# Hybrid attention and feed-forward layer on one core: the first batch element's moments, preparations, row sums and scores are placed elsewhere

## The chip, the cores and the metric

The kernel runs on one core of a Trainium2 chip. The metric is the device time of one execution in microseconds (us); the median of three runs before the change is 4003.38 us. The engines are called PE (TensorE), DVE (VectorE), ACT (ScalarE), POOL (GpSimd) and SP (SyncE, which here only issues transfers).

## The reference

The input x has 8 batch elements of 512 tokens and 256 features. Four residual layers follow each other, each on the layer norm of x:

```python
x = x + attn_a(layernorm(x))   # per token: attention between the 64 places of each of 16 heads
x = x + ffn(layernorm(x))
x = x + attn_b(layernorm(x))   # causal attention over the 512 tokens
x = x + ffn(layernorm(x))      # the same weights again

def attn_a(x):                 # H, C = 16, 64
    Q, K, V = x @ Wq + bq, x @ Wk + bk, x @ Wv + bv      # each reshaped to (b, s, H, C), Q / sqrt(C)
    scores = einsum('bshq,bshk->bshqk', Q, K)            # masked to k <= q
    w = softmax(scores)
    return einsum('bshqk,bshk->bshq', w, V).reshape(b, s, H * C) @ Wo + bo
```

The change is in attn_a of the first batch element. For every token and head, the 64 outputs are quotients of two row sums over a triangle of 64 x 64 scores: the sum of exp(q k) v, over the sum of exp(q k).

## The kernel before

**Tiles and units.** 128 tokens lie on the 128 partitions, so a batch element b has four token tiles i. Four heads (256 columns) make a column group g, so there are 16 groups (g, i) per batch element, taken with g outermost. The triangle of each head is cut into its diagonal and into squares of 32, 16, 8, 4, 2 and 1; these make four units u of work per group:

- unit 0: the 32-squares of two heads; unit 2: those of the other two heads. Scores (L784) are made by POOL from the copies kt of K and Q in SBUF.
- unit 1: the 16-squares of four heads. Scores are made by DVE, into the tile w16, of which there is one buffer.
- unit 3: all smaller squares, scores by DVE, into the tile ws, one buffer.

Units 0 and 2 use tiles w, three buffers. A unit's scores are two instructions of 128x1024 (four smaller ones in unit 3).

**Steps.** The class AttentionA lays the units of all batch elements in one list, and step(n) issues, in one fixed order, what is due at step n for several units: scores of unit n (`scores`), exponentials of unit n-1 on ACT (`exps`, L798), the product with v of unit n-2 on DVE (`weigh`, L808), a transfer that adds one half of the tile to the other (`halve`, issued by POOL, L814; not for unit 3), a further halving on POOL for units 0 and 2 (`fold`, L819), the row sums on DVE (`gather`, L845, into tiles red), and their addition on POOL into the group's sums acc (`add_rows`, L852). `small_squares` (L835, L852) adds the 2- and 1-squares. Then come the reciprocal on DVE (`invert`, L856), the product with it on POOL (`divide`, L860), the transposes and the output projection on PE. Within a group of four steps, the order that matters here is this (k is the step modulo 4; three parts to a step, separated by yields):

- k = 0: weigh unit 2; POOL's scores of unit 0, with the transfer of unit 2 between their two instructions; the reciprocal; then divide and the fold of unit 0.
- k = 1: weigh unit 3, gather unit 1; then scores of unit 1, add_rows, small_squares, fold of unit 2; then gather unit 0.
- k = 2: weigh unit 0; POOL's scores of unit 2 with unit 0's transfer between; later gather unit 2, then gather unit 3.
- k = 3: weigh unit 1 and its transfer; then scores of unit 3.

Each of PE, DVE, ACT and POOL executes in exactly this program order (a manual schedule); SP's transfers are placed by a scheduler. The first batch element's 64 steps have no other work beside them. From step 75 on, the feed-forward layers and the second attention of batch element b-1 (generator `after_a`) are issued between the parts of the steps of element b, in proportion to estimated costs.

**The start.** x of element 0 is loaded first. Then follow the rows last_qv and last_k and the weights of the column groups (fitted). `fit_qkv(g)` subtracts the last row from the weights (L344, L346; by DVE for g = 0, by POOL otherwise), puts the bias into their last row by a small transfer, and stores them in DRAM, from where `load_w` fetches them for every later group. `measure(b)` takes the four tiles' moments on DVE (L524, L525) and their scales on POOL (L529 to L532). The generator `later_weights` prepares what later layers need: a bias in three bfloat16 parts (ACT L421, L422; POOL L423; DVE L428), the scaled w3 (L451), wbqk and wbvp with their last rows subtracted (L456), their stores, and a bound on the scores (`bound_scores`: squares on ACT L373 and L374 of sqv and sk, 96 products on PE L382, a norm on ACT L388 and DVE L390). One piece of it is issued after each part of a step. Its tiles, like last_qv, last_k and the weights of groups 1 to 3, come from one pool of seven blocks of 1 MB (`block`), a block being free again after its last use.

```python
wt = ctx.enter_context(tc.tile_pool(name="wt", bufs=1))
hp = ctx.enter_context(tc.tile_pool(name="hp", bufs=7))
ps_f = ctx.enter_context(tc.tile_pool(name="ps_f", bufs=5, space=bass.MemoryType.PSUM))
```

Of the kernel before, what the change touches and what calls it, by code (L numbers as in the profile page):

```python
# [9 lines left out]
F32 = mybir.dt.float32  # L10
# [3 lines left out]
ALU = mybir.AluOpType  # L14
AX = mybir.AxisListType

P = 128
# [9 lines left out]
GW = GH * C  # L27
NG = HID // GW
# [256 lines left out]
def fast_path(ctx: ExitStack, tc: tile.TileContext, k, t, flag):  # L285

    nc = tc.nc
    ident = k.ident
# [7 lines left out]
    ap_ = ctx.enter_context(tc.tile_pool(name="ap", bufs=2))  # L296
# [42 lines left out]
    def fit_qkv(g):  # L339

        wqv, wk = fitted[g]
        eng = nc.vector if g == 0 else nc.gpsimd
        qv_last = last_qv[:, g * 2 * GW : (g + 1) * 2 * GW].unsqueeze(1).to_broadcast([P, DC, 2 * GW])
        eng.tensor_tensor(wqv, wqv, qv_last, ALU.subtract)  # L344
        k_last = last_k[:, g * GW : (g + 1) * GW].unsqueeze(1).to_broadcast([P, DC, GW])
        eng.tensor_tensor(wk, wk, k_last, ALU.subtract)  # L346
        nc.sync.dma_start(wqv[P - 1 : P, DC - 1, :], t.b_qv[g : g + 1, :])
        nc.sync.dma_start(wk[P - 1 : P, DC - 1, :], t.b_a[1:2, g * GW : (g + 1) * GW])
        nc.sync.dma_start(wqv_d[g].rearrange("p (c f) -> p c f", c=DC), wqv)
        nc.sync.dma_start(wk_d[g].rearrange("p (c f) -> p c f", c=DC), wk)  # L350
# [206 lines left out]
    def squares(unit):  # L557

        off = 0
        for n, h0, nh in unit:  # L560
            nsq = nh * C // (2 * n)
            yield n, off, nsq, slice(h0 * C, (h0 + nh) * C)
            off += nsq * n * n
# [40 lines left out]
    class AttentionA:  # L604
# [33 lines left out]
        def step(self, n):  # L638

            weighed = self.at(n - 2)  # L640
            if weighed[0] is not None:
                self.weigh(*weighed)
            unit = self.at(n)
            on_pool = unit[3] in (0, 2)
            if on_pool:
                half = self.scores(*unit)
                next(half)
            if weighed[0] is not None:
                self.halve(*weighed)
            if on_pool:  # L650
                next(half, None)
            b, i, g, u = self.at(n + 40)
            if u == 0 and g == 0 and i == 0 and b > 0:
                self.x[b] = load_x(b)
            b, i, g, u = self.at(n + 10)
            if u == 0 and g == 0 and i == 0:
                self.measure(b)
            b, i, g, u = self.at(n + 8)
            if u == 0 and g == 0:
                self.live["xn"] = normed(self.x[b][:, i, :], *self.rn[b, i], "a")  # L660
            b, i, g, u = self.at(n - 5)
            if u == NU - 1:
                self.invert(b, i, g)
            b, i, g, u = self.at(n - 4)
            if u == 1:
                self.gather(b, i, g, u)
            b, i, g, u = self.at(n + 7)
            if u == 0 and g == 0:
                nc.scalar.copy(self.live[b, i], self.live.pop("ps_ln"))
            if self.at(n - 1)[0] is not None:  # L670
                self.exps(*self.at(n - 1))
            yield
            if unit[0] is not None and not on_pool:
                for _ in self.scores(*unit):
                    pass
            for args in self.sums:
                self.add_rows(*args)
            self.sums = []
            b, i, g, u = self.at(n - 5)
            if u == NU - 1:  # L680
                self.divide(b, i, g)
            b, i, g, u = self.at(n - 2)
            if u == NU - 1:
                self.small_squares(b, i, g)

            b, i, g, u = self.at(n - 4)
            if u == 0:
                self.fold(b, i, g, u)
            b, i, g, u = self.at(n - 3)
            if u == 2:  # L690
                self.fold(b, i, g, u)
            b, i, g, u = self.at(n - 9)
            if u == NU - 1:
                self.new_x(b, i, g)
            b, i, g, u = self.at(n + 2)
            if u == 0:
                self.keep_qk(b, i, g)
            b, i, g, u = self.at(n - 7)
            if u == NU - 1:
                self.turn_group(b, i, g)  # L700
            b, i, g, u = self.at(n - 8)
            if u == NU - 1:
                self.project_out(b, i, g)
            b, i, g, u = self.at(n + 3)
            if u == 0:
                self.project(b, i, g)
            yield
            b, i, g, u = self.at(n - 4)
            if u == 2:
                self.gather(b, i, g, u)  # L710
            b, i, g, u = self.at(n - 5)
            if u == 0:
                self.gather(b, i, g, u)
            b, i, g, u = self.at(n - 3)
            if u == NU - 1:
                self.gather(b, i, g, u)
            b, i, g, u = self.at(n - 7)
            if u == NU - 1:
                nc.scalar.copy(self.live["att"], self.live.pop("pta"))
            b, i, g, u = self.at(n + 8)  # L720
            if u == 0 and g == 0:
                self.live[b, i] = lnp.tile([P, DC, P], F32, tag="xnt_a", name=f"xnta_{b}_{i}", bufs=NT)
                self.live["ps_ln"] = turned_over(self.live.pop("xn"), half_bank().rearrange("p (c s) -> p c s", c=DC))
            yield
# [40 lines left out]
        def scores(self, b, i, g, n_u):  # L765

            qv, kt = self.live[b, i, g][:2]
            if n_u == 0:
                acc = ap_.tile([P, 2, GW], F32, tag="acc", name=f"acc_{b}_{i}_{g}", bufs=3)
                self.live[b, i, g].append(acc)  # L770
                nc.vector.tensor_tensor(acc[:, 0, :], qv[:, 0], kt[:, 0], ALU.mult)

            if n_u in (0, 2):
                w = wt.tile([P, 4096], F32, tag="w", name=f"w_{b}_{i}_{g}_{n_u}", bufs=3)
            elif n_u == 1:
                w = wt.tile([P, 4096], F32, tag="w16", name=f"w16_{b}_{i}_{g}")
            else:
                w = wt.tile([P, 2 * SMALL], F32, tag="ws", name=f"ws_{b}_{i}_{g}")
            self.live[b, i, g, n_u] = w
            eng, q = (nc.gpsimd, kt[:, 1]) if n_u in (0, 2) else (nc.vector, qv[:, 0])  # L780
            for n, off, nsq, cols in squares(units[n_u]):
                for e, ev, rows, columns in pieces(w, n, off, nsq, cols):
                    shape = list(e.shape)
                    eng.tensor_tensor(  # L784
                        e, rows(q).to_broadcast(shape), columns(kt[:, 0]).to_broadcast(shape), ALU.mult
                    )
                    yield
# [50 lines left out]
        def gather(self, b, i, g, n_u):  # L838


            w = self.live.pop((b, i, g, n_u))
            for n, off, nsq, cols in squares(units[n_u]):
                if n > 2:
                    red = ap_.tile([P, 2, nsq * n], F32, tag=f"red{nsq * n}", name=f"red_{b}_{i}_{g}_{n_u}_{n}", bufs=2 + (n < 32))
                    nc.vector.tensor_reduce(red, self.columns_of(w, n, off, nsq), AX.X, ALU.add)  # L845
                    self.sums.append((b, i, g, n, cols, red))

        def add_rows(self, b, i, g, n, cols, part):

# [1 line left out]
            rows = acc[:, :, cols].rearrange("p a (x t) -> p a x t", t=2 * n)[..., n:]  # L851
            nc.gpsimd.tensor_tensor(rows, rows, part.rearrange("p a (x i) -> p a x i", i=n), ALU.add)  # L852

        def invert(self, b, i, g):
            acc = self.live[b, i, g][2]
            nc.vector.reciprocal(acc[:, 0, :], acc[:, 0, :])  # L856

        def divide(self, b, i, g):
            acc = self.live[b, i, g][2]
            nc.gpsimd.tensor_tensor(acc[:, 1, :], acc[:, 1, :], acc[:, 0, :], ALU.mult)  # L860

        def turn_group(self, b, i, g):
            acc = self.live.pop((b, i, g))[2]
# [477 lines left out]
    with tc.manual_schedule(engines={ET.PE, ET.DVE, ET.Activation, ET.Pool}):  # L1341
        a = AttentionA()
        prep = later_weights()
        fit_qkv(0)
        weights = None
        done, spent = after_a(), 0
        for n in range(-10, a.steps):
            for part, _ in enumerate(a.step(n)):
                if n >= 2:
                    next(prep, None)  # L1350
                while 3 * spent * each < total * (3 * (n - each - 11) + part + 1):
                    spent += next(done)
            if 0 <= n < NG - 1:
                fit_qkv(n + 1)
        for _ in done:
            pass
    judge()
# [86 lines left out]
```

## Time and profile before

| | us |
|---|---|
| runs | 4002.61, 4003.38, 4004.08; median 4003.38 |
| the profiled execution | 4009.55 |
| its span, first to last instruction | 4007.6 |
| first reciprocal (L856) | 86.2 |
| second | 141.4 |
| from the second on, spacing in the first batch element | 23.7 |
| sixteenth, the last of the first batch element | 475.6 |
| spacing of the later ones, mean of 111 | 28.7 |

There are 128 reciprocals, one per group, so their spacing shows the pace of the kernel. Busy time is given per engine; transfers are counted apart. A duration is that of one instruction from its start to its end, and instructions of one engine overlap a little at their ends, so that the next one can start before the last has ended: what an instruction costs its engine is read from start to start.

### The profile page before, as it was taken

What the parts mean: (1) busy time and instruction counts of PE and PEld (TensorE: products, weight loads), DVE (VectorE), ACT (ScalarE), POOL (GpSimd) and SP (SyncE); (2) the same over time, 40 slices, a digit from 0 to 9 for tenths busy, and PEclk for the clock granted to TensorE, in tenths of its full rate; (3) what the DMA queues carried; (4) which work ended last, traced back from release to release, by engine and by line L of the source; (5) the groups of instructions that cost most, each with busy time, mean ns of one, the idle gap of its engine ahead of it and who ended that gap; (6) DMA issues with size and microseconds to landing.
All of it is one profiled execution on the core that took longest, in us unless ns stands there. A gap on an engine that the chain in (4) does not pass through costs nothing.

```text
span 4007.6 us, 37678 instructions
## 1 busy us (share of the span) xinstructions
PE 2958.0 (74%) x12328; PEld 2012.2 (50%) x12328; DVE 3376.7 (84%) x3777; ACT 2337.2 (58%) x3145; POOL 3098.1 (77%) x3051
## 2 busy tenths in 40 slices
PE   1543478777876888768787788768787778768988
PEld 0311145355653656346553566346653556436847
DVE  4899988998889888998989988998889988897115
ACT  2433465666755766666755767567656667555342
POOL 6688888887888887887888888888888878886211
PEclk7555689888987989889897889879898899879999
DMA  8566777668776777668776688668877687767304
GB/s 240 114 141 145 146 182 182 147 161 199 199 162 126 195 188 196 150 147 210 174 192 139 168 198 214 147 131 198 195 181 151 154 199 205 155 133 210 126 29 167
DMA packets 118653, 671.07 MB, mean 167 GB/s; under 512 B 12704, under 2 KB 31915, under 8 KB 43824
## 3 DMA queue, kind: packets, MB, share of 16 engines
q0 software_dynamic: 78336, 570.46, 62.9%
q1 hardware_dynamic: 40112, 98.11, 6.8%
q8 instruction: 100, 1.64, 0.2%
q14 instruction: 105, 0.86, 0.1%
HBM read 255.90 MB, written 9.96 MB: 66 GB/s over the span
## 4 chain that ended last, share of the span: by engine, by line
DVE 38%; PE 16%; POOL 14%; DMA 12%; issue 8%; ACT 8%; POOLq 0%; DVEq 0%; ACTq 0%
DVE red L845 15%; DMA w<-w 12%; DVE w L808 10%; PE ph L1120 5%; ACT w L798 3%; POOL w L819 3%; DVE ws L808 3%; POOL w L784 3%; PE pqkb L1167 3%; DVE ws L784 3%; POOL acc L852 3%; DVE w L784 2%; POOL w L814 2%; DVE acc L856 2%; POOL h L1036 2%
## 5 line engine op out<-in xcount | busy, mean ns | idle before, releaser
L798 ACT ACTIVATE w<-w 128x2048 f32<-128x2048 f32 x384 | 734.2, 1913 | 653.8 <-POOL w L784 440.8
L1120 PE MATMUL ph<-h,hidden 128*128 128x512 f32 x4096 | 1047.9, 412 | 77.4 <-POOL h L1036 45.5
L784 POOL TENSOR_TENSOR w<-k 128x1024 f32<-128x1024 f32 x512 | 1076.2, 2102 | 9.6 <-ACT k L762 9.0
L1120 PEld LDWEIGHTS ph<-h,hidden 128*128 128x128 f32 x4096 | 795.3, 196 | 282.1 <-POOL h L1036 55.9
L808 DVE TENSOR_TENSOR w<-w,qv 128x1024 f32<-128x1024 f32 x768 | 899.8, 1213 | 22.4 <-ACT w L798 22.3
L845 DVE TENSOR_REDUCE red<-w 128x128 f32<-128x1024 f32 (+1 forms) x384 | 601.8, 1567 | 171.6 <-DMA w<-w 94.6
L819 POOL TENSOR_TENSOR w<-w 128x1024 f32<-128x1024 f32 x256 | 643.1, 2512 | 72.5 <-DMA w<-w 71.9
L814 POOL DMA_DIRECT2D w<-w x384 | 337.1, 878 | 339.7 <-issue 134.8
L852 POOL TENSOR_TENSOR acc<-acc,red 128x256 f32<-128x256 f32 (+1 forms) x640 | 471.0, 736 | 152.3 <-DVE red L845 124.5
L845 DVE TENSOR_REDUCE red<-ws 128x256 f32<-128x2048 f32 (+1 forms) x256 | 435.5, 1743 | 0.0
L746 PE MATMUL qv<-wqv,xnta 128*128 128x512 f32 x512 | 299.3, 715 | 89.9 <-DVE ws L808 82.4
L808 DVE TENSOR_TENSOR ws<-ws,qv 128x1024 f32<-128x1024 f32 (+3 forms) x512 | 294.7, 638 | 49.4 <-ACT ws L798 49.4
L1052 PE MATMUL pw<-xnt,gate 128*128 128x512 f32 (+2 forms) x1152 | 298.8, 419 | 24.9 <-ACT silu L1028 18.0
L784 DVE TENSOR_TENSOR w<-qv,k 128x1024 f32<-128x1024 f32 x256 | 301.3, 1219 | 3.6
L784 DVE TENSOR_TENSOR ws<-qv,k 128x1024 f32<-128x1024 f32 (+3 forms) x512 | 299.8, 648 | 0.0
L868 PE MATMUL bank<-ident,acc 128*128 128x128 f32 x256 | 64.3, 341 | 287.5 <-ACT k L761 287.1
L798 ACT ACTIVATE ws<-ws 128x1920 f32<-128x1920 f32 x128 | 231.5, 1809 | 75.3 <-DVE ws L784 74.7
L1052 PEld LDWEIGHTS pw<-xnt,gate 128*128 128x128 f32 x1152 | 227.6, 213 | 82.1 <-ACT silu L1028 22.3
L1229 ACT ACTIVATE eb<-psb 128x256 f32<-128x256 f32 (+3 forms) x512 | 182.2, 443 | 146.6 <-PE psb L1226 146.3
L1146 PE MATMUL pof<-w,h 128*128 128x256 f32 x1024 | 247.9, 396 | 19.4 <-ACT h L1085 19.4
L1085 ACT ACTIVATE h<-ph,s_sb 128x512 fp32r<-128x512 f32 (+1 forms) x256 | 171.1, 688 | 145.9 <-PE ph L1120 144.6
L856 DVE RECIPROCAL acc<-acc 128x256 f32<-128x256 f32 x128 | 223.2, 1744 | 12.3 <-POOL acc L852 12.3
(143 smaller groups left out, 4723.5 us busy)
## 6 DMA issues: line engine op xcount, KB each, us to landing
w<-w POOLq DMA_DIRECT2D x384, 1024.0 KB, 7.7
hidden<-in_h POOLq DMA_DIRECT2D x128, 1024.0 KB, 7.9
gate<-in_w12p POOLq DMA_DIRECT2D x32, 1024.0 KB, 9.0
w<-w_d SPq DMA_DIRECT2D x16, 1024.0 KB, 12.0
wqv<-wqv_d SPq DMA_DIRECT2D x31, 512.0 KB
wo<-in_wo SPq DMA_DIRECT2D x32, 256.0 KB, 7.4
wbqk<-wbqk_d SPq DMA_DIRECT2D x8, 1024.0 KB
w<-in_h SPq DMA_DIRECT2D x8, 1024.0 KB, 7.0
```

Source lines behind the costliest of these rows:

```text
L746: nc.tensor.matmul(qv.rearrange("p j f -> p (j f)"), xnt[:, c, :], wqv[:, c, :], start=(c == 0), stop=(c == DC - 1),)
L784: eng.tensor_tensor(e, rows(q).to_broadcast(shape), columns(kt[:, 0]).to_broadcast(shape), ALU.mult)
L798: nc.scalar.activation(e, e, AF.Exp, scale=C**-0.5)
L808: nc.vector.tensor_tensor(ev, e, columns(qv[:, 1]).to_broadcast(list(e.shape)), ALU.mult)
L814: nc.gpsimd.dma_start(w[:, :2048], w[:, 2048:], accum_op=ALU.add)
L819: nc.gpsimd.tensor_tensor(w[:, :1024], w[:, :1024], w[:, 1024:2048], ALU.add)
L845: nc.vector.tensor_reduce(red, self.columns_of(w, n, off, nsq), AX.X, ALU.add)
L852: nc.gpsimd.tensor_tensor(rows, rows, part.rearrange("p a (x i) -> p a x i", i=n), ALU.add)
L856: nc.vector.reciprocal(acc[:, 0, :], acc[:, 0, :])
L1052: nc.tensor.matmul(pj[:, toks], w[:, m % 4, j, c, :], xs[:, p, c, toks], start=(p == 0 and c == 0), stop=(p == 1 and c == DC - 1),)
L1120: nc.tensor.matmul(pss[j], w[:, j, c, :], h_in(p, c), start=(p == 0 and c == 0), stop=(p == 1 and c == MC - 1),)
L1146: nc.tensor.matmul(po, h(0, c)[:, i * P : (i + 1) * P], w3[:, c, :], start=(c == 0), stop=False)
```

## The change

- `measure(0)` is issued ahead of `fit_qkv(0)`, and no longer at step -10.
- `fit_qkv` of the groups 1, 2 and 3 is issued after the steps 3, 13 and 23 instead of 0, 1 and 2; the pieces of `later_weights` are issued from step 5 on instead of step 2.
- For batch element 0 (`alone`), the scores of unit 1 are made by POOL from kt.
- For batch element 0, `sum_up` adds the row sums in PSUM: five products with the identity on PE, of acc and of the four tiles red. `invert` and `divide`, now both on DVE, read them there.
- The tiles red hold the sums of all four heads for one size of square, so those of units 0 and 2 go into one tile of 128x256, with one buffer; the three other sizes have three buffers. For the other batch elements POOL adds both halves in one instruction, so that there are four additions of red in a group and not five.

```diff
@@ step
             b, i, g, u = self.at(n + 10)
             if u == 0 and g == 0 and i == 0:
-                self.measure(b)
+                if b > 0:
+                    self.measure(b)
...
             if u == 0:
                 self.project(b, i, g)
+            b, i, g, u = self.at(n - 4)
+            if u == NU - 1 and self.alone(b):
+                self.sum_up(b, i, g)
             yield
@@ scores
             eng, q = (nc.gpsimd, kt[:, 1]) if n_u in (0, 2) else (nc.vector, qv[:, 0])
+            if n_u == 1 and self.alone(b):
+                eng, q = nc.gpsimd, kt[:, 1]
@@ gather
                 if n > 2:
-                    red = ap_.tile([P, 2, nsq * n], F32, tag=f"red{nsq * n}", name=f"red_{b}_{i}_{g}_{n_u}_{n}", bufs=2 + (n < 32))
-                    nc.vector.tensor_reduce(red, self.columns_of(w, n, off, nsq), AX.X, ALU.add)
-                    self.sums.append((b, i, g, n, cols, red))
+                    if n_u != 2:
+                        self.live["red", n] = ap_.tile(
+                            [P, 2, GW // 2], F32, tag=f"red{n // 32}", name=f"red{n}_{b}_{i}_{g}", bufs=1 if n == 32 else 3
+                        )
+                    red = self.live["red", n]
+                    part = red[:, :, cols.start // 2 : cols.stop // 2]
+                    nc.vector.tensor_reduce(part, self.columns_of(w, n, off, nsq), AX.X, ALU.add)
+                    if n_u != 0 and not self.alone(b):
+                        self.sums.append((b, i, g, n, slice(0, GW), red))
@@ new, and invert and divide
+        @staticmethod
+        def alone(b):
+
+            return b == 0
+
+        def sum_up(self, b, i, g):
+
+            sums = ps_f.tile([P, 2, GW], F32, tag="pf", name=f"sums_{b}_{i}_{g}")
+            nc.tensor.matmul(sums, ident, self.live[b, i, g][2], start=True, stop=False)
+            for n in (32, 16, 8, 4):
+                rows = sums.rearrange("p a (x t) -> p a x t", t=2 * n)[..., n:]
+                red = self.live["red", n].rearrange("p a (x i) -> p a x i", i=n)
+                nc.tensor.matmul(rows, ident, red, start=False, stop=n == 4)
+            self.live[b, i, g].append(sums)
+
         def invert(self, b, i, g):
-            acc = self.live[b, i, g][2]
-            nc.vector.reciprocal(acc[:, 0, :], acc[:, 0, :])
+            acc, *sums = self.live[b, i, g][2:]
+            nc.vector.reciprocal(acc[:, 0, :], sums[0][:, 0, :] if sums else acc[:, 0, :])
 
         def divide(self, b, i, g):
-            acc = self.live[b, i, g][2]
-            nc.gpsimd.tensor_tensor(acc[:, 1, :], acc[:, 1, :], acc[:, 0, :], ALU.mult)
+            acc, *sums = self.live[b, i, g][2:]
+            if sums:
+                nc.vector.tensor_tensor(acc[:, 1, :], sums[0][:, 1, :], acc[:, 0, :], ALU.mult)
+            else:
+                nc.gpsimd.tensor_tensor(acc[:, 1, :], acc[:, 1, :], acc[:, 0, :], ALU.mult)
@@ the main loop
         prep = later_weights()
+        a.measure(0)
         fit_qkv(0)
...
             for part, _ in enumerate(a.step(n)):
-                if n >= 2:
+                if n >= 5:
                     next(prep, None)
...
-            if 0 <= n < NG - 1:
-                fit_qkv(n + 1)
+            if n in (3, 13, 23):
+                fit_qkv(n // 10 + 1)
```

## The prediction

> **What bounds the kernel now.** I read the page first, then busy time by stage, then one period of the first batch element in order of time.
>
> ```profile
> span 4007.6 us, 37678 instructions
> PE 2958.0 (74%) x12328; PEld 2012.2 (50%) x12328; DVE 3376.7 (84%) x3777; ACT 2337.2 (58%) x3145; POOL 3098.1 (77%) x3051
> DVE 38%; PE 16%; POOL 14%; DMA 12%; issue 8%; ACT 8%; POOLq 0%; DVEq 0%; ACTq 0%
> ```
>
> No engine is full over the whole span, so the stages have to be read apart. The change acts in the first two: the start, and the rest of the first element's attention, which has no feed-forward work beside it. The columns are the stretch, its length, then busy us (count) of PE, PEld, DVE, ACT and POOL, the granted clock, the DMA share and GB/s.
>
> ```profile
> 52.00:92.00 40.00, 5.90 (x12) 2.96 (x12) 25.82 (x27) 10.51 (x10) 38.95 (x37) 0.54 0.98 287
> 92.00:113.00 21.00, 2.94 (x14) 2.92 (x14) 0.32 (x1) 5.85 (x6) 1.88 (x1) 0.50 0.55 151
> 150.00:500.00 350.00, 139.55 (x245) 66.08 (x246) 349.38 (x361) 138.09 (x142) 305.05 (x268) 0.56 0.68 141
> ```
>
> From 150 to 500 us DVE is idle for 0.6 of 350 us: DVE bounds this stage. A group (four steps) takes 23.72 us, the spacing of the reciprocals (L856) from 141.4 us on; the sixteenth is at 475.6. From 92 to 113 us everything waits for one load:
>
> ```profile
> ACT sk L374 <- DMA sk<-in_wqkv: 21.9, 1, 21.9
> ```
>
> One stretch of the periodic stage, in order of time (start, duration, engine, line, out<-in; other rows left out):
>
> ```profile
> 311.31 2.28 DVE L845 TENSOR_REDUCE red<-w 128x256 f32<-128x2048 f32 x1
> ...
> 313.62 2.36 DVE L784 TENSOR_TENSOR w<-qv,k 128x1024 f32<-128x1024 f32 x2
> 313.73 0.81 POOL L852 TENSOR_TENSOR acc<-acc,red 128x256 f32<-128x256 f32 x1
> 314.42 0.69 POOL L835 TENSOR_TENSOR ws<-ws 128x256 f32<-128x256 f32 x1
> 315.19 1.66 POOL L852 TENSOR_TENSOR acc<-acc,ws 128x256 f32<-128x256 f32 x2
> ...
> 316.80 2.36 POOL L819 TENSOR_TENSOR w<-w 128x1024 f32<-128x1024 f32 x1
> ...
> 317.35 2.34 DVE L808 TENSOR_TENSOR w<-w,qv 128x1024 f32<-128x1024 f32 x2
> ...
> 319.61 1.21 DVE L845 TENSOR_REDUCE red<-w 128x128 f32<-128x1024 f32 x1
> ```
>
> Rows 1 and 2: DVE reduces unit 1's tile w16 and at once refills it with the next group's scores; w16 has one buffer. The last reduce needs POOL's fold of unit 2, which ends at 316.80 + 2.36 = 319.16, only 0.45 us before DVE starts on it. DVE leads, but POOL is close behind in this one place.
>
> **What the Trainium skill says.** GPSIMD Engine Reference, 3.1 Elementwise: a two-input operation takes 1.96 times as long as on VectorE; here a score piece advances POOL by 1.92 us and DVE by 1.13, 1.7 times. TensorE: Matmul & The Clock Gate, Architectural detail, calls ACT, DVE and GPSIMD strict FIFOs; the trace agrees in that every period repeats one order per engine, so what is put ahead of the fold delays the fold. DMA: Bandwidth & Descriptors, Issuing engines are not separate DMA queues: transfers from any engine share the 16 DMA engines; 52 to 92 us agrees, with share 0.98 while SP's and POOL's transfers run together. Perfetto Trace Analysis, Optimization Strategy: "Consistent bubbles" can mean that there isn't room for the next tile; before, DVE has none here. I expect them after.
>
> **Periodic stage, by work.** Steps from start to start. DVE loses unit 1's scores (313.62 to 315.90, 2.28) and gains the product that was L860 on POOL (the PSUM-reading 128x256 product L805 advances DVE by 0.33): 23.72 - 1.95 = 21.77. POOL has one gap of 2.68 us in a period (before the DMA issue at 303.21), so 21.04 of work; it gains 2 x 1.92 = 3.84 and loses five adds (3.7) and the product L860 (0.69): about 20.5. By work alone DVE would still bound, at 21.77.
>
> **Periodic stage, by waits.** In the step with unit 1, scores come first in POOL's part, ahead of small_squares and the fold of unit 2. Now they are POOL's, and write w16, so they wait until DVE's reduce of the group before has ended (311.31 + 2.28 = 313.59). From there: 0.07 to start (the add at 117.30 came 0.07 after its reduce), scores 3.84, L835 0.77, two adds 1.61, fold 2.35: it ends 8.64 after the reduce, at 322.23. DVE, rid of its scores, would want it after 1.12 + 0.33 + 2.26 = 3.7 us, at about 317.3. Stall: 4.9 us a period.
>
> The loop closes on DVE: reduce of unit 2 1.13, of unit 3 3.32, weighing of unit 1 2.26, scores of unit 3 2.26, weighing of unit 2 2.26, L771 0.33, reciprocal 1.66, product 0.33, weighing of unit 3 2.20, reduce of unit 1 2.28; sum 18.03; with POOL's 8.64 and 0.03 to start, **26.70 us against 23.72: +2.98 a group**. The queue behind the waiting POOL instruction is the small squares, the fold, unit 2's scores and the DMA issue; DVE waits for the fold. Unit 2's exponentials, next in line, would end some 4 us before they are used. The trace doesn't show POOL's price for the 16x16 shape: at least 1.82, at most the 2.10 that a whole piece of unit 0 or 2 is recorded with, so 26.5 to 27.1; I take 1.92, as the piece has as many elements and the same innermost run of 8.
>
> Groups: unit 1 is POOL's for 16 groups, which gives 15 such waits; the first two fall before the twelfth step, in the start counted below. 13 x 2.98 = **+38.7**; the last interval, without the wait but with the lighter DVE, gives back 1.
>
> **Sums on TensorE.** A 128x512 product with the identity 1.04 us, four of 128x256 at 0.66: 3.7 us a group. PE is busy 140 of 350 us, and between the end of DVE's last reduce (324.14) and the reciprocal (331.3) lie 7 us, of which the two last products need 1.3. Cost 0; were PE's cover gone, 3.7 less those 7, still 0. Reading sums from PSUM: L805 (0.41, PSUM) and its like L771 (0.42) cost the same; up to 0.1 a group. The PSUM pool's five buffers are hardly used here.
>
> **Other batch elements.** One add for both halves of the 32-squares: 112 adds of 0.69 us (77 us of POOL) go, but on the chain they carry 2.3 us, in five of 112 groups, so at most -2.3; the single buffer costs nothing, as at least 10.1 us lie between the add and the next write (rows L852 and L845 in order of time). I take -1, bounds -2.3 and +1.
>
> **The start.** Moments: x is there at 2.98, the four pairs take 2.2 us and POOL's scaling 2.0, all under DVE's 10.4 us wait for wqv. But projection then waits for the fitted weights' bias row, issued on SP at 17.11; with some 2 us to land (x needs 2.5), it starts at about 19.5 instead of 22.43: -2.9. Then three fits (3 x 3.7 on POOL) no longer stand ahead of unit 2's scores. My run by hand: k at 25.0, unit 0's scores to 28.9, unit 1's to 32.7, unit 2's to 37.5, exponentials to 39.5: DVE's first weighing of unit 2 at 39.6 instead of 50.95, **-11.3** (the 2.9 is in it). Each moved fit also issues on SP two bias rows and stores of 0.5 and 0.25 MB; the loads of the stored weights come at steps 9, 25 and 41, the fits at 3, 13 and 23, so at least six steps of some 6 us lie between: cost 0.
>
> The preparations come later and cost again. Their six casts and three subtractions alternate between ACT and POOL and hold DVE up for about 9 us. last_qv, last_k and two fit blocks now stay until steps 13 and 23, so of the seven blocks three are left for four: wbvp must wait for w3's store before it can load. SP and POOL queue behind: I count 8 us of waiting on POOL for w3 and wbvp. rows, w3, wbqk, wbvp, their stores and the squares move 8.75 MB at some 260 GB/s, beside 1 MB for each halving, so sk lands near 118 us and holds ACT at step 10 (before: 107 us, at step 7). The second reciprocal comes at about 127.6 instead of 141.4: **-13.8**, all of the above included. After it fall the norm's wait (L390, 3.98, and two table loads of 1.28: 5 net) and the second fit (3.7 less 2.3 of slack: +1.4); the third hides in POOL's gap. Start: **-7.4**, bounds -25 (all stalls overlap) and +15 (each block is waited for in turn).
>
> **Sum.** -7.4 + 38.7 - 1 - 1, less 1 for a hiccup of 2.1 us near 400 us that the bubbles absorb: **+28**. The profiled execution took 4009.55 us (its span 4007.6 and 1.95 around it), 6.2 above the median 4003.38; +28 gives 4037.6 there and **4031** as a median.
>
> **Rivals.** *The lighter DVE wins:* if unit 1's scores did not wait, or the fold came in time, the period would be 21.77: 16 x -1.95 = -31, with the start -38, 3965 us. For it: POOL's work does fit. Against it: w16's one buffer and the fold's 0.45 us. It decides at a fold ending 3.7 us after the reduce, 8.64 by my count. 9%. *The start gets worse* by the shortage of blocks: +15 for -7.4, 4054 us; for it, the load of sk already stalls for 21.9 us. 14%. *The start absorbs it:* most of the old 31.5 us between the first two reciprocals (55.2 less 23.7) and the 11.3 vanish: -38, with +36 after it, about 4001. The full DMA share speaks against it. 9%. My forecast, 68%.
>
> **Numbers.** 0.2%, 8 us, is about what a measurement of this kernel tells from no change. Faster by more: the first rival and a little of the third, 0.10; within: 0.08; slower: 0.82. Range 4010 to 4052: the start's bounds and the shape's price, short of the two far cases.
>
> **What will show it.** After, DVE's reduces (L845) wait for POOL's fold (L819) by about 5 us once a group in the first element, reciprocals stand 26.7 apart, POOL's scores wait for DVE's reduce, and nothing waits for TensorE's sums. The second reciprocal lies near 128 us. I am wrong if the reciprocals stand at 21.8, or if the fold isn't what DVE waits for.

## The result and the profile after

The changed kernel is slower: 4045.36 us (median of four runs, 4043.04 to 4055.76) against 4003.73 us, ratio 1.0101, 95% interval 1.0074 to 1.0129. Forecast were 4031 us, in a range from 4010 to 4052. The profiled execution took 4043.04 us, its span is 33.7 us longer than that of before. The page of the changed kernel (whose line numbers are higher from line 657 on) has these lines for those shown of before:

```profile
span 4041.3 us, 37835 instructions
PE 2994.3 (74%) x12488; PEld 2034.5 (50%) x12488; DVE 3348.9 (83%) x3761; ACT 2336.3 (58%) x3145; POOL 3083.0 (76%) x2875
DVE 34%; POOL 22%; PE 17%; DMA 11%; issue 9%; ACT 8%; SPq 0%; POOLq 0%; ACTq 0%; DVEq 0%
```

DVE and POOL both have less to do, and still the kernel is longer: POOL's share of the chain has risen from 14% to 22%. Busy time by stage, columns as before (the busy us of DVE is the third of the five pairs, that of POOL the fifth):

```profile
92.00:113.00 21.00, 0.69 (x2) 0.29 (x2) 6.78 (x6) 2.44 (x3) 14.37 (x12) 0.50 0.51 164
150.00:500.00 350.00, 176.26 (x382) 95.21 (x382) 286.28 (x313) 123.69 (x126) 281.09 (x191) 0.66 0.62 130
```

In the stage that DVE filled to 349.38 of 350 us it now sits idle for 64 us. One period there, in order of time:

```profile
311.30 3.40 DVE L856 TENSOR_REDUCE red<-w 128x256 f32<-128x2048 f32 x2
...
313.65 3.86 POOL L790 TENSOR_TENSOR w<-k 128x1024 f32<-128x1024 f32 x2 [1.26 <-DVE red L856]
...
317.47 0.61 POOL L841 TENSOR_TENSOR ws<-ws 128x256 f32<-128x256 f32 x1
...
318.16 1.66 POOL L864 TENSOR_TENSOR acc<-acc,ws 128x256 f32<-128x256 f32 x2
...
319.78 2.34 POOL L825 TENSOR_TENSOR w<-w 128x1024 f32<-128x1024 f32 x1
...
322.15 1.22 DVE L856 TENSOR_REDUCE red<-w 128x128 f32<-128x1024 f32 x1 [4.86 <-POOL w L825]
```

The brackets give an engine's idle time and who ended it. POOL's scores of unit 1 wait for DVE's reduce of the tile that they overwrite (here the row's first 2.28 us); the small squares and the fold of unit 2 queue behind them; DVE waits 4.86 us for the fold. The waits from 150 to 500 us have it in twelve groups, ten times with 4.9 us, once each with 4.6 and 2.7 (the thirteenth, of 0.7 us, is for another fold); the columns are us in total, times, and the longest:

```profile
DVE red L856 <- POOL w L825: 56.7, 13, 4.9
POOL w L790 <- DVE red L856: 18.3, 12, 4.5
```

The reciprocals divide the spans. Traces of all runs, in us (the tail is from the last reciprocal on):

| kernel | third reciprocal at | third to sixteenth | sixteenth to last | tail |
|---|---|---|---|---|
| before | 165.1 | 310.5 | 3212.8 | 319.2 |
| before, once more | 160.4 | 310.5 | 3218.3 | 319.3 |
| changed | 172.4 | 346.4 | 3201.1 | 321.3 |
| scores_last | 172.5 | 333.6 | 3202.0 | 322.6 |
| scores_dve | 164.8 | 317.4 | 3203.1 | 321.6 |
| old_start | 177.1 | 345.9 | 3208.2 | 318.0 |
| old_start_last | 176.0 | 334.6 | 3203.6 | 316.3 |
| start_only | 171.3 | 313.9 | 3214.2 | 319.1 |
| prep_later_only | 148.8 | 310.5 | 3222.9 | 320.7 |
| merge_only | 162.5 | 310.5 | 3201.8 | 319.7 |
| two_adds_late | 162.4 | 310.7 | 3203.2 | 322.0 |
| merge_prep | 147.0 | 310.5 | 3197.6 | 320.8 |
| scores_last_no_transfer | 169.6 | 301.5 | 3208.0 | 321.6 |

So the 33.7 us of the changed kernel are +7.3, +35.9, -11.7 and +2.1. The two traces of before lie 4.7 us apart at the third reciprocal and 5.5 us apart in the long stretch, so a difference of that size between two single traces shows nothing. The ratios below compare medians with runs of before taken along with each experiment; those gave 4011.04, 4011.14 or 4011.84 us.

### The profile page after: what moved, and what is told of

Read it like the earlier page. It is cut to its first block, busy times and chain, and to the rows that moved or that the text cites. A ratio compares the mean times of both kernels' runs of the same rounds, so it can differ in the third digit from the quotient of the medians.

```text
span 4041.3 us, 37835 instructions
## 1 busy us (share of the span) xinstructions
PE 2994.3 (74%) x12488; PEld 2034.5 (50%) x12488; DVE 3348.9 (83%) x3761; ACT 2336.3 (58%) x3145; POOL 3083.0 (76%) x2875
## 4 chain that ended last, share of the span: by engine, by line
DVE 34%; POOL 22%; PE 17%; DMA 11%; issue 9%; ACT 8%; SPq 0%; POOLq 0%; ACTq 0%; DVEq 0%
DVE red L856 13%; DMA w<-w 10%; DVE w L814 9%; POOL w L790 5%; PE ph L1150 5%; POOL w L825 5%; POOL acc L864 4%; ACT w L804 3%; PE pqkb L1197 3%; DVE ws L790 3%; DVE ws L814 2%; POOL w L820 2%; POOL h L1066 2%; DVE acc L883 2%; DVE w L790 2%
## 5 line engine op out<-in xcount | busy, mean ns | idle before, releaser
L790 POOL TENSOR_TENSOR w<-k 128x1024 f32<-128x1024 f32 x544 | 1144.1, 2106 | 36.1 <-DVE red L856 18.3
L864 POOL TENSOR_TENSOR acc<-acc,red 128x256 f32<-128x256 f32 x448 | 368.0, 821 | 106.2 <-DVE red L856 81.5
L1082 PE MATMUL pw<-xnt,gate 128*128 128x512 f32 (+2 forms) x1152 | 289.5, 409 | 27.3 <-ACT silu L1058 19.8
L790 DVE TENSOR_TENSOR w<-qv,k 128x1024 f32<-128x1024 f32 x224 | 263.6, 1218 | 3.0
L1176 PEld LDWEIGHTS pof<-w,h 128*128 128x128 f32 x1024 | 196.9, 194 | 57.8 <-ACT h L1115 24.8
```

What stands on the lines that cost most here:

```text
L790: eng.tensor_tensor(e, rows(q).to_broadcast(shape), columns(kt[:, 0]).to_broadcast(shape), ALU.mult)
L1082: nc.tensor.matmul(pj[:, toks], w[:, m % 4, j, c, :], xs[:, p, c, toks], start=(p == 0 and c == 0), stop=(p == 1 and c == DC - 1),)
L1176: nc.tensor.matmul(po, h(0, c)[:, i * P : (i + 1) * P], w3[:, c, :], start=(c == 0), stop=False)
```

## Experiments on the first element's stage

**scores_last.** The changed kernel with unit 1's scores moved in `step`:

```diff
-            if unit[0] is not None and not on_pool:
+            if unit[0] is not None and not on_pool and not (unit[3] == 1 and self.alone(unit[0])):
                 for _ in self.scores(*unit):
                     pass
...
             if u == 2:
                 self.fold(b, i, g, u)
+            if unit[0] is not None and unit[3] == 1 and self.alone(unit[0]):
+                for _ in self.scores(*unit):
+                    pass
```

> The changed kernel, with one thing moved: for the first batch element the scores of unit 1 are issued on GpSimd after small_squares and the fold of unit 2, not ahead of them. If the loop through the fold is what costs (my theory), the fold no longer waits for VectorE's reduce; the loop that is left goes from the reduce through 3.84 us of scores, 4.8 of unit 2's scores and issue, 1.9 of exponentials back to VectorE's weighing, about 20 us, so VectorE's own work bounds: spacing of the reciprocals 21.8 us instead of 26.8, no wait of the reduces for the fold, some 13 x 5 = 65 us less than the changed kernel, about 3975 to 3985 us. If GpSimd simply has too much work or the 16x16 shape is dear there (rival 1), the order doesn't matter: 26 to 27 us, 4040. If the sums on TensorE delay the reciprocal (rival 2), also 26.8.

Measured: 4033.0 us, 1.0051 (1.0031 to 1.0071) of before; 25.8 us a group on the mean from the third to the fifteenth reciprocal, against 26.8. The order matters, so rivals 1 and 2 fall as they were put, but only by 1.0 us, and my 21.8 was missed by 4 us. This run alone doesn't decide for the loop through the fold; scores_dve and the count of the loop do more for it. Against an overloaded POOL speaks that it is busy for 281.09 of 350 us in the changed kernel. The waits of scores_last from 200 to 480 us show what took the place of the old one:

```profile
POOL w L828 <- DMA w<-w: 27.9, 11, 4.6
DVE red L859 <- POOL w L828: 18.4, 10, 3.5
DVE w L817 <- ACT w L807: 12.8, 11, 1.2
```

The fold now waits for the transfer of unit 2, which cannot be issued before DVE has weighed unit 2; with the scores behind the fold, that closes a second loop, which I had left out. DVE also waits 12.8 us for the exponentials of unit 1, whose scores now come later.

**scores_last_no_transfer.** The same, and for the first element this transfer left out, so that its sums there lack half of unit 2's terms:

```diff
-            if n_u < NU - 1:
+            if n_u < NU - 1 and not (n_u == 2 and self.alone(b)):
```

> The changed kernel with unit 1's scores after the fold, and for the first batch element the transfer of unit 2 left out, so that half of that unit's terms is missing from the sums there. The run with the scores after the fold gave 25.7 us a group where I expected 21.8; its trace has the fold waiting for this transfer. If the loop through the transfer (weighing of unit 2, transfer, fold, unit 1's and unit 2's scores, exponentials) bounds that run, this one is bound by VectorE: 21.8 to 22.4 us a group. If GpSimd's work or the sums bound it, it stays at 25 to 26.

Measured: 23.1 us a group (277.2 us for twelve), with groups between 22.2 and 24.0; 4002.58 us in one run. Leaving out the transfer takes 2.7 of the 25.8 us away; 23.1 lies above the range expected for DVE alone. From 200 to 480 us (busy columns as above) DVE is idle for 9.9 us, and two waits make up 8.2 of them:

```profile
200.00:480.00 280.00, 140.85 (x323) 76.88 (x321) 270.11 (x288) 111.59 (x116) 243.37 (x161) 0.67 0.51 108
DVE acc L886 <- PE sums L881: 4.7, 5, 1.4
DVE red L859 <- DMA w<-w: 3.5, 3, 1.7
```

So DVE's own work is 22.3 us a group (23.1 times 270.11 / 280), and in this order the reciprocal (L886) does wait for TensorE's sums, in five groups: rival 2 has a small part here. Why the sums come late there wasn't tested.

**scores_dve.** The changed kernel without the two lines in `scores`:

```diff
-            if n_u == 1 and self.alone(b):
-                eng, q = nc.gpsimd, kt[:, 1]
```

> The changed kernel with unit 1's scores of the first batch element on VectorE again; sums on TensorE and the new start stay. My theory: VectorE bounds with 23.72 + 0.33 for the product it took over, spacing 24.05 us, the sums cost nothing; the start alone makes the difference to before, the total within +-12 us of before. Rival 2 (TensorE's sums delay the reciprocal): spacing stays near 26.8 and the total near 4040. Rival 1 (GpSimd overloaded) expects 24.05 as well.

Measured: 24.24 us in ten of the twelve groups; 4015.38 us, 1.0008 (0.9998 to 1.0018) of before. Giving unit 1 back to DVE takes away the whole loss of the stage but 0.52 us a group. DVE is busy again all the time, which rules out a wait for TensorE's sums in this order (columns as above, 200 to 480 us):

```profile
200.00:480.00 280.00, 145.57 (x311) 78.01 (x311) 279.00 (x295) 106.24 (x112) 201.90 (x143) 0.68 0.68 142
```

**old_start and old_start_last.** The changed kernel, and scores_last, with the start of before:

```diff
-                if b > 0:
-                    self.measure(b)
+                self.measure(b)
...
-        a.measure(0)
...
-                if n >= 5:
+                if n >= 2:
...
-            if n in (3, 13, 23):
-                fit_qkv(n // 10 + 1)
+            if 0 <= n < NG - 1:
+                fit_qkv(n + 1)
```

> The changed kernel with the start as before: measure(0) at step -10, fits after steps 0 to 2, preparations from step 2. The first element's scores and sums stay changed. My theory: spacing 26.8 us as in the changed kernel; the second reciprocal near 141 to 147 us, as the start before gave it (141.4) plus up to two waits for the fold; so the new start as a whole is worth between 0 and -8 us at the third reciprocal (172.4 in the changed kernel), total 4040 to 4050. If the new start is what made the kernel slower (rival 3), this one is faster than the changed kernel by 10 us or more.

> Both: the start as before and unit 1's scores after the fold. My theory: spacing 21.8 us from the second reciprocal (about 140 us), the sixteenth near 140 + 14 x 21.8 = 445 instead of 475.6 before, total about 3970 to 3978 us, faster than before. With the fold's loop not the cause: 26.8 and 4040.

Measured: old_start 4050.22 us, 1.0093 (1.0074 to 1.0112), again 26.80 us a group: the new start is not what made the kernel slower. The second reciprocal, at 150.3 us, came later than the 141 to 147 expected. The third is 4.7 us later than in the changed kernel, no more than the two traces of before differ, so what the new start is worth beside the new scores isn't shown. old_start_last 4037.14 us, 1.0068 (1.0047 to 1.0088): again about 25.8 a group, so its expectation failed with that of scores_last.

## Experiments on the start

**start_only** and **prep_later_only** put moves of the start into the kernel before. The first has all three (the last diff turned round); the second leaves the fits where they were:

```diff
-                self.measure(b)
+                if b > 0:
+                    self.measure(b)
...
+        a.measure(0)
...
-                if n >= 2:
+                if n >= 5:
```

> The kernel before with the three moves of the start alone: moments ahead, preparations from step 5, fits after steps 3, 13 and 23. VectorE bounds with 23.72 us a group as before. From the variant with VectorE's scores (third reciprocal 164.8 us, with the dearer product) I expect the third reciprocal at 160 to 165 us, against 165.1 before, and a total 0 to 5 us less than before. The prediction's count for the start would give about 158.

> As the one with the moves of the start alone, but the fits after steps 0 to 2 as before, so that all seven blocks are free when the preparations begin. If the shortage of blocks holds sk back (it is issued at 118.8 us in the changed kernel, when the store of wbvp has landed), sk is issued earlier, before 105 us, and the third reciprocal comes some 10 us sooner than with late fits. If the DMA rate is the limit, sk lands at about the same time as in the changed kernel, 130 us, and the third reciprocal doesn't come sooner.

Measured: start_only 4023.02 us, 1.0038 (1.0024 to 1.0051): slower, against what I expected, third reciprocal 171.3. prep_later_only 3997.07 us, 0.9965 (0.9952 to 0.9978): faster, third reciprocal 148.8, as a shortage of blocks would have it. The late fits alone cost 26 us between the medians, 22.5 of them in the traces by the third reciprocal, more than the other two moves gain. The rows of the line that loads sk show the shortage of blocks (the row with the semaphore is SP coming to the load, the other the load going out). In start_only SP comes to it at 105.9 us and waits; the load goes out at 115.9, and ACT stands 15.2 us for it (14.5 in the changed kernel):

```profile
L370 SPq EVENT_SEMAPHORE  x1: 17/17/17, 105.9 to 105.9; - x1
L370 SPq DMA_DIRECT2D sk<-in_wqkv x1: 379/379/379, 115.9 to 115.9; - x1
  ACT sk L374: 15.2, 1
```

In the changed kernel the chain (start, duration, what) has the load following the landing of wbvp's store, to the hundredth of a us:

```profile
108.34 10.46 DMA wbvp_d<-wbvp
118.81 11.21 DMA sk<-in_wqkv
```

In prep_later_only SP finds the block free, the load goes out 42 us earlier than in start_only, and the same view has no engine waiting for it:

```profile
L370 SPq EVENT_SEMAPHORE  x1: 28/28/28, 73.7 to 73.7; - x1
L370 SPq DMA_DIRECT2D sk<-in_wqkv x1: 1098/1098/1098, 73.7 to 73.7; - x1
```

## Experiments on the other batch elements

**merge_only.** The kernel before with the tiles red of the change and one addition for both halves, in all elements (the diff of `gather`, with `if n_u != 0:` for its last condition).

> The kernel before, with nothing changed but the tiles of the row sums: units 0 and 2 share one tile, and GpSimd adds both halves in one instruction, in all batch elements. The prediction's step: the removed additions carry 2.3 us of the chain, so the time is within 3 us of before. Against it: in the changed kernel and four variants the stretch from the sixteenth reciprocal to the last is 3201 to 3208 us, against 3212.8 before, so the merge could be worth about 10 us: then about 3995 when before gives 4004, ratio 0.9975.

> The kernel before once more, for a second trace. If the 10 us by which the stretch from the sixteenth to the last reciprocal differs are the merge's, this trace has about 3212 us again; if they are scatter between executions, it can lie between 3201 and 3213.

Measured: merge_only 3991.87 us, 0.9953 (0.9939 to 0.9966), 19 us less. before_again has 3218.3 us from the sixteenth reciprocal to the last; the four traces without the merge or the move lie between 3212.8 and 3222.9, the nine with one of them between 3197.6 and 3208.2. So it was not scatter, and my 2.3 us were wrong.

**two_adds_late.** Still two additions, the first issued with the second:

```diff
-                    self.sums.append((b, i, g, n, cols, red))
+                    if n_u == 0:
+                        self.live["first"] = (b, i, g, n, cols, red)
+                    else:
+                        if n_u == 2:
+                            self.sums.append(self.live.pop("first"))
+                        self.sums.append((b, i, g, n, cols, red))
```

> The kernel before, with unit 0's addition still an instruction of its own, but issued with unit 2's, one step later. As many instructions and as much work on GpSimd as before; only the place is that of the merged one. If what helped in the merge is that no addition stands between unit 2's scores and unit 1's transfer (the place), this gives most of its gain, a ratio of 0.9955 to 0.998. If it is the 0.7 us less work on GpSimd per group, it gives none, 0.999 to 1.001.

Measured: 3997.8 us, 0.9964 (0.9949 to 0.9978). With all of POOL's work back, 14 of the 19 us stay: most of the gain is the place. The intervals of the two runs overlap, so the rest isn't shown to be the saved work. Before, the addition stood between POOL's last scores of unit 2 and the transfer of unit 1. DVE's reduces from 500 to 3680 us (after the bars: busy us and mean ns of one; then the idle time before them and what ended it), first of before, then of merge_only:

```profile
L845 DVE TENSOR_REDUCE red<-w 128x256 f32<-128x2048 f32 x332 | 520.6, 1568 | 160.8 <-DMA w<-w 87.3 <-POOL w L819 73.3
```

```profile
L850 DVE TENSOR_REDUCE red<-w 128x256 f32<-128x2048 f32 x333 | 521.9, 1567 | 150.2 <-POOL w L819 80.1 <-DMA w<-w 70.1
```

Waiting for transfers falls from 87.3 to 70.1 us (70.3 in two_adds_late), while waiting for the fold rises a little. The transfer of unit 1 is issued as soon after its weighing as before (0.6 us on the mean of 112) but lands after 8.47 us instead of 8.69 (two_adds_late has 8.47 us too, the second trace of before 8.69). Why the earlier POOL eases the transfers wasn't settled.

**merge_prep.** What helped, together: merge_only with the diff of prep_later_only.

> The kernel before with what the earlier runs showed to help, and nothing of what cost: one tile and one addition for the 32-squares' sums in all batch elements (0.9953), moments ahead and preparations from step 5 with the fits after steps 0 to 2 (0.9965). The two act in different stages (after the sixteenth reciprocal; before the third), so the gains should add: about 19 + 14 = 33 us less than before, ratio 0.992, third reciprocal near 149 us, spacing 23.72, about 3978 us when before gives 4011. If they share a cause, it is nearer 0.995.

Measured: 3978.78 us, 0.9922 (0.9909 to 0.9935), third reciprocal 147.0: faster than both kernels, and the gains add as expected.

## Why the prediction was right

- **The loop through the fold: right.** 26.70 us a group were summed, 26.80 measured; the stall of 4.9 us was 4.86; the fold was to end 8.64 us after the reduce and ends after 8.54 (322.12 less 313.58). The price of the 16x16 shape, the unseen term, was as taken: two pieces advance POOL by 3.82 us (313.65 to 317.47); for the 1.82 a piece given as its lower bound no working is on record. One term of the sum was wrong: the last interval did not give back 1 us but cost 0.5 (24.24), since DVE makes the scores of the next element's unit 1 in it. The Trainium skill, Perfetto Trace Analysis, Optimization Strategy, says that the same gap repeating on an engine that should be saturated can mean that there isn't room for the next tile. It fits in part: DVE's gap of 4.9 us comes back group after group, and POOL's scores wait for a tile with one buffer, but DVE itself waits for another tile, through POOL's queue. A second buffer wasn't tried; whether it or the order is the better cure stays open.
- **By work alone DVE would bound at 21.77: never seen,** since scores_last meets another loop first. The rival of the lighter DVE would have needed both removed; even the run without the transfer has 23.1, of which 22.3 are DVE's own work.
- **Sums on TensorE: nearly right.** Counted 24.05 with DVE's product, measured 24.24 in scores_dve. No wait in the changed kernel and in scores_dve, but the product follows the reciprocal that it reads, 1.78 us from start to start, where the sum had 1.66. Cost 0 holds for these orders only: in scores_last_no_transfer DVE waits 4.7 us for the sums.
- **The start: the sign was wrong.** Forecast were 127.6 us for the second reciprocal and, with 26.7 and 6.4 after it, 160.7 for the third; measured are 141.9 and 172.4. The failed term is the landing of sk, counted at 118 us and seen at 130, which is 12 of the 14.3 us: the store of wbvp (issued at 108.3) took 10.5 us and sk, which waited for its block, 11.2; both ran beside 2 MB of sqv. The cause, three blocks left for four tiles, was named and is seen in the traces; its size was put too low, which made the second rival half true.
- **Other batch elements: wrong.** "On the chain they carry 2.3 us, so at most -2.3": merge_only gave 19 us less. The share of the chain was taken as a bound on the gain, and it was none: with the addition out of the way, DVE's waits for transfers fell by 17 us, and why isn't settled.

The start's +11.7 against the forecast and the other elements' -10.7 nearly cancelled. That was luck: neither size was foreseen. What is left of the total rests on the loop: +28 us were forecast; +33.5 lie between the two profiled executions and +41.6 between the medians.

## What to carry over

Before giving work to an engine with slack, follow its queue: what stands behind the moved instruction, what it waits for, and whether the engine that is relieved waits for something in that queue. Sum the loop, not the work. When a preparation is spread out, count the buffers that it keeps occupied; and don't take an instruction's share of the chain as a bound on what moving it can gain.

## What was not expected

An addition of 0.7 us, once in a group, on an engine that is busy 77% of the time was worth 14 us over the whole kernel when moved by one step, work unchanged: 4011.84 to 3997.8 us. And moving three fits of 3.7 us out of the busy start cost 22.5 us at the third reciprocal; the traces put it down to the blocks that their inputs held.
